# A Mamba block beside a two-layer local transformer: P's transposes in row halves, and six summed groups of eight

## The chip, the cores and the metric

The kernel runs on one core of a Trainium2 chip. The core has TensorE (PE, whose weight loads are shown as PEld), VectorE (DVE), ScalarE (ACT), GpSimd (POOL) and SyncE (SP), which issues nearly all DMAs here. The metric is the time of one execution on the device in microseconds (us). Everything is computed in float32.

## The reference

The input x has 4096 tokens of 256 features. Two branches read it, and the result is the sum that the kernel forms from x and both branches' contributions.

The Mamba branch, on the normalized tokens: a projection to 512 inner channels and a gate, a causal convolution of 4 taps with SiLU, then a state of 16 numbers per channel:

```
dt  = softplus(dt_lr @ dt_w.T + dt_b)
dA  = exp(dt * A)                     # per channel and state
h_t = dA_t * h_(t-1) + dt * x_conv * B
y_t = sum over the 16 states of h_t * C_t
out = ((y + x_conv * D) * silu(z)) @ out_w.T
```

The transformer branch has two layers. In each, tokens are shifted by half of their features and projected to q, k and v of 8 heads of 64. q and k are normalized and rotated. Attention is local: a window of 128 queries sees its own 128 keys and the 128 before, with a mask. After it come an output projection with a residual, a layer norm and a gated MLP.

```
sim  = q @ k.T                        # 128 x 256 per head and window, masked
attn = softmax(sim)                   # "P" below
o    = attn @ v
```

## The kernel before

**Tiling.** A transformer step handles 256 tokens (two windows) of one layer; there are 16 steps in each of 2 layers. The Mamba branch goes in 8 blocks of 512 tokens, each in 4 chunks of 128 channels: 32 chunk-blocks, one beside each transformer step. All of it is one program in which the instructions of both branches are interleaved.

**What sets the order.** Each operation is handed to a planner by `add(engine, us, emit, reads, writes, ..., soon=...)`. `us` is the duration that the planner assumes, and `soon` is a lead: the operation's due time is moved ahead by it (or back, where it is negative). A list scheduler then plays the five engines and picks on each the operation that is due first among those whose inputs and buffers are ready. `AHEAD` says how far ahead of the oldest unfinished work an operation may be due to be considered. For PE, `part` says how the array is used: the whole of it (""), two halves of its rows ("rows") or of its columns ("columns"). The planner charges `SWITCH` (0.1) for a change and prefers work of the same part within `NEAR` (0.3). The resulting order is written out for each engine and is fixed: an engine does not pass a waiting instruction. All of SP's DMAs stand in one such order too.

**Mamba's states** (`recur`, L772 on). A chunk-block takes its 16 states in 8 groups of two. For each group SP loads two 512 KB buffers (`bc`, seven in all) with B and C spread over the partitions. GpSimd multiplies B by dt*x (L793, 128x1024). For each of the two states ACT computes the decay (L802), DVE scans (L807) and multiplies by C into the first buffer (L817). The sum over states is taken by PE: four transposes of 128x128 a state accumulate into one PSUM bank `y` (L829). In groups named in `PAIRED` GpSimd adds the two states first (L825), and PE has four transposes instead of eight. `PAIRED` is (1, 3, 5, 7). `close` copies y out and finishes the chunk.

**Attention** (`attend`, `pair(g)`). A window's 8 heads go in two pairs of head pairs, g = 0 and 1. For each g:

- `score` (L1017): products for four heads with contraction 64, two at a time in the halves of the array's rows, into two PSUM banks.
- `masked` (L1032, DVE): mask, scale and row maximum. `soft` (L1042, ACT): exponential and row sum, into the SBUF tiles `prs[j]`, each with queries as partitions and two heads x 256 keys.
- `turn` (L1055): P's transposes, 128x128, so that the keys become partitions. It is done for each head pair i on its own: four transposes (two heads, two pieces of keys) into one PSUM bank, whole array.
- an ACT copy of each bank into an SBUF tile `prT` (L1059; four tiles in all).
- `mix` (L1071): products with v, two at a time in halves of the columns.

Five PSUM banks named `mm` serve all products of both branches, two hold decays and one holds `y`. A float32 product that isn't a transpose leaves two records in the trace for one written instruction; a transpose leaves one.

Of the kernel before, what the change touches and what calls it, by code (L numbers as in the profile page):

```python
# [42 lines left out]
AHEAD = 2.32  # L43
# [5 lines left out]
PAIRED = (1, 3, 5, 7)  # L49
# [269 lines left out]
def mamba_and_local_transformer(  # L319
# [45 lines left out]
    probs_T = buffer("prT", 4, [P, 2, 2, P])  # L365
# [89 lines left out]
    def load_small():  # L455
        dma(96, lambda: xpw.ap, lambda: xp_wT.rearrange("(c p) n -> p c n", p=P), writes=[xpw], soon=-0.84)
        for at_row in (0, DH):
            dma(32, lambda at_row=at_row: dtw.ap[at_row : at_row + DTR], lambda: dt_wT, writes=[(dtw, at_row)], soon=-0.13)
        dma(128, lambda: b2row.ap, lambda: b2_d[DEPTH - 1 : DEPTH, :].partition_broadcast(P), writes=[b2row], soon=-0.82)

    def load_qkv(l):
        for s in range(3):
            cut = slice(s * INNER, (s + 1) * INNER)
            dma(
                512, lambda cut=cut: wqkv.ap[:, :, cut],
                lambda cut=cut: wqkv_d[l][:, cut].rearrange("(k p) n -> p k n", p=P), writes=[(wqkv, s)], soon=-0.17,
            )

    def load_rest(l):
        dma(512, lambda: wo.ap, lambda: wo_d[l].rearrange("(h p) n -> p h n", p=P), writes=[wo], soon=0.41)  # L470
        for half in range(2):
            for m, n in ((0, WHOLE), (NM - 1, LAST)):
                to, of = w1_at(half, m), half * HID + m * MC
                dma(
                    n, lambda to=to, n=n: w1.ap[:, :, to : to + n],
                    lambda of=of, n=n: w1_d[l][:, of : of + n].rearrange("(k p) n -> p k n", p=P),
                    writes=[(w1, (half, m))], soon=-1.5,
                )
# [3 lines left out]
            lambda: w2_d[l][0:whole, :].rearrange("(m p) n -> p m n", p=MC), writes=[(w2, 0)], soon=0.34,  # L482
        )
        dma(42, lambda: w2.ap[0 : HID - whole, NM - 1, :], lambda: w2_d[l][whole:HID, :], writes=[(w2, 1)], soon=0.91)
# [28 lines left out]
        add("PE", 8.3, shift, [w1], [pb], soon=-0.76)  # L513
        add("DVE", 0.4, bias, [pb], [b1, b1x], soon=-0.11)
        add("DVE", 4.6, scale, [], [w1], port=True, soon=-1.45)
# [14 lines left out]
    def base_of(s):  # L530

        base = plan.value(rows_b)
        if s in sums:
            dma(256, lambda: base.ap, lambda: sums[s].ap, [sums[s]], [base], soon=-0.77)
            return base
        dma(256, lambda: base.ap, lambda: rows(x, s), writes=[base], soon=-1.13)
# [3 lines left out]
            ), [b2row], [base], soon=-0.58,  # L540
# [3 lines left out]
    def finish(s, po, base):  # L544

        add("DVE", 0.6, lambda: nc.vector.tensor_tensor(base.ap, halves(po), base.ap, ALU.add), [po], [base], soon=-1.06)
        if s in sums:
            dma(256, lambda: rows(out, s), lambda: base.ap, [base], soon=-0.55)
            return
        sums[s] = plan.fixed(dram.tile([P, NW, D], F32, tag=f"sum{s}", name=f"sum{s}"))  # L550
        dma(256, lambda: sums[s].ap, lambda: base.ap, [base], [sums[s]], soon=-1.4)
# [4 lines left out]
    def shift_column(l, s):  # L556
        now = xts[l, s]
        if s == 0:
            add("POOL", 0.14, lambda: nc.gpsimd.memset(now.ap[:, 1, 0:1], 0.0), [], [(now, 0)], soon=-0.51)
        else:  # L560
# [3 lines left out]
                [(old, 1)], [(now, 0)], soon=-0.73,  # L564
            )

    def normalize(s):
# [5 lines left out]
        dma(256, lambda: xb.ap, lambda: rows(x, s), writes=[xb], soon=0.15)  # L573
# [27 lines left out]
        add("DVE", 1.1, stats, [xb], [mv], soon=1.5)  # L601
        add("ACT", 0.5, root, [mv], [rstd], soon=0.26)
        add("DVE", 0.6, centre, [mv, rstd], [xb], port=True, soon=0.02)
        now = xts[0, s] = plan.value(tokens)
        add("PE", 0.44, turn, [xb], [pt], holds=[now], soon=0.92)
        add("ACT", 0.48, lambda: nc.scalar.copy(now.ap[:, :, 1:], halves(pt)), [pt], [(now, 1)], soon=0.26)
        shift_column(0, s)
        dma(256, lambda: xn_d[s].ap, lambda: now.ap[:, :, 1:], [(now, 1)], [xn_d[s]], soon=0.98)
# [3 lines left out]
    def reload(s):  # L612
        now = xts[1, s] = plan.value(tokens)
        dma(256, lambda: now.ap[:, :, 1:], lambda: x1_d[s].ap, [x1_d[s]], [(now, 1)], soon=0.04)
        shift_column(1, s)
# [5 lines left out]
    def in_half(i):  # L621
# [3 lines left out]
            lambda: in_wT[:, i * DI : (i + 1) * DI].rearrange("(k p) n -> p k n", p=P), writes=[w], soon=-1.17,  # L625
# [3 lines left out]
    def in_proj(b, w, c, to):  # L629
# [9 lines left out]
        add("PE", 1.72, emit, [w, xms[b]], [pm], holds=[to], soon=-0.68)  # L639
        return pm  # L640

    def front_load(b):
        xm = xms[b] = plan.value(xms_b)
        for i in range(PB):
            s = b * PB + i
            dma(
                256, lambda i=i: xm.ap[:, :, i * TS : (i + 1) * TS], lambda s=s: xn_d[s].ap, [xn_d[s]], [(xm, i)], soon=0.54
# [5 lines left out]
    def front_conv(b, c, w):  # L653
        xin, xc, tail = plan.value(rows_m), xcs[b], tails[b]
        edge = slice(c * (TAPS - 1), (c + 1) * (TAPS - 1))
        if b == 0:
            add("POOL", 0.14, lambda: nc.gpsimd.memset(xin.ap[:, 0 : TAPS - 1], 0.0), [], [(xin, 0)], soon=-0.13)
        else:
# [3 lines left out]
                [(old, c)], [(xin, 0)], soon=0.95,  # L662
            )
        pm = in_proj(b, w, c, xin)
        add("ACT", 0.48, lambda: nc.scalar.copy(xin.ap[:, TAPS - 1 :], pm.ap), [pm], [(xin, 1)], soon=1.39)
        if b < NB - 1:
            add(
                "POOL", 0.14, lambda: nc.gpsimd.tensor_copy(tail.ap[:, edge], xin.ap[:, TB:]), [(xin, 1)], [(tail, c)], soon=-0.13
# [5 lines left out]
            ), [], [pm], soon=-1.0,  # L674
# [8 lines left out]
        for j in range(TAPS - 1):  # L683
            add("DVE", 0.7, lambda j=j: tap(j), [xin, pm], [(xc, c) if j == TAPS - 2 else pm], soon=1.04)

    def silu(v):
# [4 lines left out]
        add("ACT", 4.52, emit, [], [v], soon=0.84)  # L691

    def front_dbl(b):
# [3 lines left out]
        def emit():  # L697
# [9 lines left out]
        add("PE", 1.75, emit, [xc, xpw], [px], holds=[xd, part], soon=-0.37, part="columns")  # L707
        add("ACT", 0.48, lambda: nc.scalar.copy(part.ap[0:n, 0:TB], px.ap[DH : DH + n]), [px], [part], alone=[px], soon=-0.04)
        add(
            "DVE", 0.6, lambda: nc.vector.tensor_tensor(xd.ap[0:n], px.ap[0:n], part.ap[0:n, 0:TB], ALU.add),  # L710
            [px, part], [(xd, 0)], alone=[px], soon=-1.5,
        )

        add("ACT", 0.48, lambda: nc.scalar.copy(xd.ap[DH : DH + DTR], xd.ap[0:DTR]), [(xd, 0)], [(xd, 1)], soon=-0.52)
        xds[b] = xd
        bc = bcs[b] = plan.fixed(dram.tile([2 * NS, TB], F32, tag=f"bc{b}", name=f"bc{b}"))
        dma(64, lambda: bc.ap, lambda: xd.ap[DTR:n, :], [(xd, 0)], [bc], soon=-0.16)
# [8 lines left out]
    def times(b, c):  # L726
# [12 lines left out]
        add("PE", 1.15, emit, [xd, dtw], banks2, holds=dts2, soon=1.25, part="rows")  # L739
        for i in range(2):  # L740
# [3 lines left out]
                ), [banks2[i]], [dts2[i]], soon=0.16,  # L744
# [3 lines left out]
    def prepare(b, c):  # L748

        if c % 2 == 0:  # L750
# [7 lines left out]
        add("ACT", 0.6, lambda: nc.scalar.activation(e.ap[:, n], dt.ap, AF.Abs), [dt], [e], soon=-0.49)  # L758
        add("ACT", 0.6, lambda: nc.scalar.activation(dt.ap, dt.ap, AF.Relu), [], [dt], soon=-1.5)
        add("ACT", 0.54, lambda: nc.scalar.activation(e.ap[:, n], e.ap[:, n], AF.Exp, scale=-1.0), [], [e], soon=0.5)  # L760
        add(
            "DVE", 0.36, lambda: nc.vector.tensor_scalar(r.ap[:, n], e.ap[:, n], 1.0, -1.0, ALU.add, ALU.add),
            [e], [r], port=True, soon=-0.19,
        )
        add("POOL", 1.22, lambda: nc.gpsimd.tensor_tensor(r.ap[:, n], e.ap[:, n], r.ap[:, n], ALU.subtract), [e], [r], soon=-0.36)
        add("ACT", 0.6, lambda: nc.scalar.activation(e.ap[:, n], e.ap[:, n], AF.Ln, bias=one_t), [], [e], soon=-0.3)
        add("POOL", 1.22, lambda: nc.gpsimd.tensor_tensor(dt.ap, dt.ap, r.ap[:, n], ALU.add), [r], [dt], soon=-1.41)
        add("POOL", 1.22, lambda: nc.gpsimd.tensor_tensor(dt.ap, dt.ap, e.ap[:, n], ALU.add), [e], [dt], soon=-0.94)
        add(
            "DVE", 0.61, lambda: nc.vector.tensor_tensor(dtx.ap, dt.ap, xc.ap[:, c, :], ALU.mult),  # L770
            [dt, (xc, c)], [dtx], port=True, soon=0.7,
# [3 lines left out]
    def recur(b, c, g):  # L775
# [6 lines left out]
        for s in range(2):  # L782
# [4 lines left out]
                .rearrange("n t -> (n t)").partition_broadcast(P), [bc], [w], soon=-0.76,  # L787
# [7 lines left out]
            ), [dtx], [u], soon=-0.28,  # L795
        )
        for i in range(NG):
# [6 lines left out]
                ), [dt], [h], soon=0.0,  # L804
# [4 lines left out]
                ), [(u, i), (state, (c, n))], [h], soon=-1.02,  # L809
            )  # L810
            if b < NB - 1:
                add(
                    "ACT", 0.1, lambda h=h, n=n: nc.scalar.copy(state.ap[:, c, n : n + 1], h.ap[:, TB - 1 : TB]),  # L813
                    [h], [(state, (c, n))], alone=[h], soon=0.11,
# [4 lines left out]
                ), [h, spread[1]], [(u, i)], alone=[h], soon=-0.32,  # L819
# [4 lines left out]
        if n_sums == 1:  # L824
            add("POOL", 1.22, lambda: nc.gpsimd.tensor_tensor(u.ap[:, 0, :], u.ap[:, 0, :], u.ap[:, 1, :], ALU.add), [], [u], soon=-1.1)  # L825
# [13 lines left out]
        for i in range(n_sums):  # L839
            add("PE", 0.44, lambda i=i: collect(i), [(u, i)], [y], soon=-0.01)  # L840

    def close(b, c):
# [3 lines left out]
        add("ACT", 0.48, lambda: nc.scalar.copy(ytv(), y.ap), [y], [yt], soon=-0.43)  # L846

        def turn():
# [3 lines left out]
        add("PE", 0.44, turn, [yt], [py], soon=-0.55)  # L852
# [3 lines left out]
            ), [py], [(xc, c)], soon=-0.04,  # L856
# [3 lines left out]
            [sz], [(xc, c)], soon=-0.23,  # L860
        )

    def out_load():
# [3 lines left out]
            writes=[w], soon=-1.42,  # L867
# [3 lines left out]
    def out_proj(b, i, w):  # L871
# [12 lines left out]
        add("PE", 3.44, emit, [w, xc, base], [po], soon=-1.12)  # L884
# [5 lines left out]
    def rotation(l, s):  # L890
# [3 lines left out]
            writes=[rot], soon=-0.47,  # L894
        )
        for i, scales in enumerate((qks, qkw)):
            for q in range(2):
# [6 lines left out]
                    ), [rot], [(trig, (i, q))], soon=-0.44,  # L904
# [3 lines left out]
    def project(l, s, t):  # L908
# [3 lines left out]
        def matmuls(q, holds):  # L912
# [10 lines left out]
            add("PE", 1.72, emit, [xb, (wqkv, q)], [pm], holds=holds, soon=0.27)  # L923
# [4 lines left out]
        def norm(q, pm, sq):  # L928
            add("ACT", 0.48, lambda: nc.scalar.activation(sq.ap, pm.ap, AF.Square), [pm], [sq], alone=[pm], soon=0.56)
# [3 lines left out]
                ), [sq], [(nrm, q)], soon=-0.65,  # L933
# [10 lines left out]
        def turned(parts, to):  # L944
            add("POOL", 1.22, lambda: nc.gpsimd.tensor_tensor(parts[0].ap, parts[0].ap, parts[1].ap, ALU.add), [parts[1]], [parts[0]], soon=0.5)  # L945
# [476 lines left out]
```

## Time and profile before

| | |
|---|---|
| median of 3 runs | 1888.05 us (1886.05 to 1889.43) |
| profiled execution | 1890.55 us, its span 1888.8 us |
| mean granted TensorE clock | 0.992 |
| DVE L807, the scans | 448 x 1279 ns, 563.7 us |
| POOL L793, products with B | 256 x 2368 ns, 605.7 us |
| ACT L1059, copies of the transposed P | 256 x 595 ns, 133.9 us |
| PE L1017, scores | 2016 records, 135.4 us busy |
| SP waiting for L829 / L817 to release a buffer | 499.4 / 645.5 us |
| DMA | 334.69 MB, 177 GB/s |

A group line of the page has: line, engine, operation, what is written from what, shapes and count; then busy time and the mean duration of one in ns; then the engine's idle time just before such instructions and what ended most of it. PE's instructions are pipelined, so their mean duration is a latency and not the distance from one to the next.

### The profile page before, as it was taken

Reading aid. Unit: us, or ns where it says so; the run is one execution under the profiler, and the core shown is the slowest. Engines: PE = TensorE matmul, PEld = TensorE weight load, DVE = VectorE, ACT = ScalarE, POOL = GpSimd, SP = SyncE. Lnnn points to the kernel's source line nnn. Section 1 sums busy time; section 2 is a strip of 40 time slices with the busy share of each in tenths; the row PEclk is TensorE's granted clock in tenths of the full one; section 3 lists DMA queues with packets and bytes.
Section 4 is the critical chain, followed back from the end, with each engine's and each line's share of the span. In section 5 each row is a group of like instructions: output and inputs, shape, how many; then the busy total and the mean of one; then the engine's idle time right before and its main releaser. Section 6 shows DMA issues by size and latency. Waiting matters only on the chain. (4 is left out here: it accounts for less than half of the span.)

```text
span 1888.8 us, 35786 instructions
## 1 busy us (share of the span) xinstructions
PE 1850.9 (98%) x12432; PEld 1422.4 (75%) x12432; DVE 1667.1 (88%) x3030; ACT 1588.7 (84%) x3794; POOL 1508.6 (80%) x1274
## 2 busy tenths in 40 slices
PE   7999999999999999999999999999999999999997
PEld 4777767777777777778778787787778777787886
DVE  6688898899898999988899888989889898899886
ACT  5788888888898888897896979988798888988793
POOL 4578778887887778887888787988788987798885
PEclk9899999999999999999999999999999999999999
DMA  5354555565455555556555554556544575455564
GB/s 189 125 193 131 171 167 167 178 209 179 157 176 190 181 179 185 164 186 208 166 186 204 181 191 147 187 170 209 176 147 171 176 248 169 144 173 175 193 197 142
DMA packets 133956, 334.69 MB, mean 177 GB/s; under 512 B 13468, under 2 KB 57200, under 8 KB 133776
## 3 DMA queue, kind: packets, MB, share of 16 engines
q1 hardware_dynamic: 133488, 332.21, 53.1%
q8 instruction: 98, 1.61, 0.3%
q14 instruction: 82, 0.67, 0.1%
q10 hardware_dynamic: 288, 0.20, 0.0%
HBM read 315.06 MB, written 17.30 MB: 176 GB/s over the span
## 5 line engine op out<-in xcount | busy, mean ns | idle before, releaser
L793 POOL TENSOR_TENSOR bc<-dtx,bc 128x1024 f32<-128x1024 f32 x256 | 605.7, 2368 | 80.7 <-DMA bc<-bc 44.7
L807 DVE TENSOR_TENSOR_SCAN da<-da,state,bc 128x512 f32<-128x512 f32 x448 | 563.7, 1279 | 56.6 <-ACT da L802 32.8
L802 ACT ACTIVATE da<-dt,negA 128x512 f32<-128x512 f32 x512 | 349.2, 698 | 49.7 <-DVE bc L817 47.9
L918 PE MATMUL mm<-wqkv,xt 128*128 128x512 f32 x768 | 353.5, 598 | 1.4 <-DVE top L1032 0.8
L817 DVE TENSOR_TENSOR bc<-da,bc 128x512 f32<-128x512 f32 x512 | 338.3, 679 | 5.8 <-ACT state L813 3.7
L1176 PE MATMUL mm<-hn,w 128*128 128x256 f32 (+1 forms) x1408 | 329.2, 381 | 2.1 <-DVE top L1032 0.7
L1176 PEld LDWEIGHTS mm<-hn,w 128*128 128x128 f32 (+1 forms) x1408 | 256.1, 188 | 39.1 <-DVE top L1032 1.6
L1042 ACT ACTIVATE pr<-pr,top 128x256 f32<-128x256 f32 (+1 forms) x512 | 253.3, 501 | 10.6 <-DVE top L1032 10.4
L918 PEld LDWEIGHTS mm<-wqkv,xt 128*128 128x128 f32 x768 | 139.7, 191 | 137.0 <-issue 121.2
L1032 DVE CUSTOM_DVE_ANT_0 pr<-mm,maskf,nrm 128x256 f32<-128x256 f32 (+1 forms) x512 | 212.4, 473 | 14.5 <-PE mm L1017 13.7
L825 POOL TENSOR_TENSOR bc<-bc 128x512 f32<-128x512 f32 x128 | 165.3, 1291 | 71.5 <-DVE bc L817 65.2
L829 PE MATMUL y<-ident,bc 128*128 128x128 f32 x1536 | 219.6, 277 | 2.2 <-ACT m2k L846 1.5
L985 POOL TENSOR_TENSOR turn<-turn,trig 128x512 f32<-128x512 f32 x128 | 162.4, 1288 | 74.0 <-DVE turn L978 63.0
L829 PEld LDWEIGHTS y<-ident,bc 128*128 128x128 f32 x1536 | 177.1, 141 | 58.6 <-issue 40.0
L945 POOL TENSOR_TENSOR turn<-turn,turn 128x512 f32<-128x512 f32 x128 | 164.2, 1283 | 32.4 <-DVE turn L965 31.4
L1017 PEld LDWEIGHTS mm<-kT,qT 64*128 64x128 f32 x2016 | 119.7, 187 | 30.9 <-issue 21.9
L1221 POOL TENSOR_TENSOR mlp<-mlp,ga 128x512 f32<-128x512 f32 (+2 forms) x128 | 127.2, 1008 | 19.1 <-ACT ga L1233 10.0
L1059 ACT COPY prT<-mm 128x512 f32<-128x512 f32 (+1 forms) x256 | 133.9, 595 | 3.4 <-PE mm L1055 3.1
L1017 PE MATMUL mm<-kT,qT 64*128 64x128 f32 x2016 | 135.4, 280 | 0.0
L1071 PE MATMUL mm<-prT,v 128*64 128x128 f32 x2016 | 134.5, 281 | 0.0
L1071 PEld LDWEIGHTS mm<-prT,v 128*64 128x64 f32 x2016 | 113.8, 137 | 25.1 <-issue 8.8
L1055 PE MATMUL mm<-ident,pr 128*128 128x128 f32 x1008 | 130.5, 276 | 2.0 <-ACT qT L956 0.9
(132 smaller groups left out, 3499.4 us busy)
## 6 DMA issues: line engine op xcount, KB each, us to landing
bc<-bc SPq DMA_DIRECT2D x512, 512.0 KB, 4.5
io<-in_x SPq DMA_DIRECT2D x32, 256.0 KB, 5.4
mw<-in_in_wT SPq DMA_DIRECT2D x16, 512.0 KB, 4.8
rot<-in_rot SPq DMA_DIRECT2D x32, 128.0 KB, 4.2
xn<-xt SPq DMA_DIRECT2D x16, 256.0 KB, 3.6
xm<-xn SPq DMA_DIRECT2D x16, 256.0 KB, 4.4
x<-mid SPq DMA_DIRECT2D x16, 256.0 KB, 4.6
mw<-in_out_wT SPq DMA_DIRECT2D x8, 512.0 KB, 6.1
```

Source lines behind the costliest of these rows:

```text
L793: "POOL", 2.35, lambda: nc.gpsimd.tensor_tensor(u.ap, dtx.ap.unsqueeze(1).to_broadcast([P, NG, TB]), u.ap, ALU.mult), [dtx], [u], soon=-0.28,
L802: "ACT", 0.63, lambda h=h, n=n: nc.scalar.activation(h.ap, dt.ap, AF.Exp, scale=negA[:, c * NS + n : c * NS + n + 1]), [dt], [h], soon=0.0,
L807: "DVE", 1.18, lambda h=h, n=n, i=i: nc.vector.tensor_tensor_scan(h.ap, h.ap, u.ap[:, i, :], state.ap[:, c, n : n + 1] if b else 0.0, ALU. ...
L817: "DVE", 0.61, lambda h=h, i=i: nc.vector.tensor_tensor(u.ap[:, i, :], h.ap, spread[1].ap[:, i, :], ALU.mult), [h, spread[1]], [(u, i)], a ...
L825: add("POOL", 1.22, lambda: nc.gpsimd.tensor_tensor(u.ap[:, 0, :], u.ap[:, 0, :], u.ap[:, 1, :], ALU.add), [], [u], soon=-1.1)
L829: nc.tensor.matmul(y.ap[:, t, :], lhsT=u.ap[:, i, t * P : (t + 1) * P], rhs=ident, is_transpose=True, start=g == 0 and i == 0 and t == 0, ...
L918: nc.tensor.matmul(pm.ap, lhsT=hT[k], rhs=wqkv.ap[:, k, q * INNER : (q + 1) * INNER], start=k == 0, stop=k == KC - 1,)
L1017: nc.tensor.matmul(halves(scs[j])[:, i, a * WIN : (a + 1) * WIN], lhsT=qT.ap[half, 2 * g + i, :], rhs=kk.ap[half, 2 * g + i, :], start=n == 0,
L1032: nc.vector.tensor_tensor_reduce(out=prs[j].ap[:, i, keys], in0=halves(scs[j])[:, i, keys], in1=mask[:, keys], scale=nrm.ap[:, h : h + 1], ...
L1042: nc.scalar.activation(prs[j].ap[:, i, keys], prs[j].ap[:, i, keys], AF.Exp, bias=top.ap[:, h : h + 1], scale=-1.0, accum_out=den.ap[:, h ...
L1071: nc.tensor.matmul(hpair(po.ap)[j * DH : (j + 1) * DH, hp, :], lhsT=vv.ap[:, h * DH : (h + 1) * DH], rhs=prT.ap[:, j, a, :], start=a == first,
L1176: nc.tensor.matmul(halves(pm)[0:r, i, :], lhsT=w1.ap[:, k, c0 : c0 + r], rhs=hn.ap[:, k, :], start=k == 0, stop=k == KC - 1,)
```

## The change

P's transposes: `turn` now handles both head pairs of a g in one piece of work. Each transpose of 128 queries x 128 keys becomes two of 64 queries x 128 keys, one in each half of the array's rows (partitions 0 to 63 and 64 to 127), written to two different banks. Bank r holds the queries of half r for both head pairs, both heads and both pieces of keys. The two ACT copies each take one bank and write every 64-query half into one wide `prT` (two tiles of twice the size instead of four). The planner's price for the turn is 0.62 as a "rows" piece, where it was twice 0.44 for the whole array.

Sums: `PAIRED` gets the groups 0 and 4, so GpSimd adds in six groups of eight. `AHEAD` goes from 2.32 to 2.82. The leads (`soon`) of nearly every operation are set anew; no operation is added or removed by that.

```diff
-AHEAD = 2.32
+AHEAD = 2.82
...
-PAIRED = (1, 3, 5, 7)
+PAIRED = (0, 1, 3, 4, 5, 7)
...
-    probs_T = buffer("prT", 4, [P, 2, 2, P])
+    probs_T = buffer("prT", 2, [P, 2, 2, 2, P])
...
-            prTs = []
-            for i in range(2):
-                pp, prT = plan.value(banks), plan.value(probs_T)
-                ppv = lambda pp=pp: pp.ap.rearrange("p (j a q) -> p j a q", j=2, a=2)
-
-                def turn(i=i, ppv=ppv):
+            pps, prT = [plan.value(banks) for _ in range(2)], plan.value(probs_T)
+            ppv = lambda r: pps[r].ap.rearrange("p (i j a q) -> p i j a q", i=2, j=2, a=2)
+
+            def turn():
+                for i in range(2):
                     for j in range(2):
                         for a, _, _ in pieces:
-                            nc.tensor.transpose(ppv()[:, j, a, :], prs[j].ap[:, i, a * WIN : (a + 1) * WIN], ident)
-
-                add("PE", 0.44, turn, prs, [pp], holds=[prT], soon=0.0)
+                            for r in range(2):
+                                half = slice(r * DH, (r + 1) * DH)
+                                nc.tensor.transpose(
+                                    ppv(r)[:, i, j, a, :], prs[j].ap[half, i, a * WIN : (a + 1) * WIN], ident[half, half]
+                                )
+
+            add("PE", 0.62, turn, prs, pps, holds=[prT], soon=1.35, part="rows")
+            for r in range(2):
                 add(
-                    "ACT", 0.48, lambda ppv=ppv, prT=prT: nc.scalar.copy(prT.ap[:, :, first:], ppv()[:, :, first:]),
-                    [pp], [prT], soon=0.27,
+                    "ACT", 0.48, lambda r=r: nc.scalar.copy(
+                        prT.ap[:, :, :, first:, r * DH : (r + 1) * DH], ppv(r)[:, :, :, first:, :]
+                    ), [pps[r]], [(prT, r)], soon=1.4,
                 )
...
             add(
-                "PE", 1.0, mix, prTs + [vv for _, _, vv in pieces], [(po, g)], holds=[] if g else [OT], soon=1.25,
+                "PE", 1.0, mix, [prT] + [vv for _, _, vv in pieces], [(po, g)], holds=[] if g else [OT], soon=0.0,
                 part="columns",
             )
```

## The prediction

> **What bounds the kernel now.** I read the page's engine shares first, then busy time and granted clock in windows of 200 us, then what TensorE waited for, then TensorE's instructions in order of time.
>
> ```profile
> PE 1850.9 (98%) x12432; PEld 1422.4 (75%) x12432; DVE 1667.1 (88%) x3030; ACT 1588.7 (84%) x3794; POOL 1508.6 (80%) x1274
> ...
> L829 PE MATMUL y<-ident,bc 128*128 128x128 f32 x1536 | 219.6, 277 | 2.2 <-ACT m2k L846 1.5 <-POOL bc L825 0.7
> ...
> L825 POOL TENSOR_TENSOR bc<-bc 128x512 f32<-128x512 f32 x128 | 165.3, 1291 | 71.5 <-DVE bc L817 65.2 <-DVE nrm L972 4.0 <-DVE den L1088 2.1
> ...
> L1055 PE MATMUL mm<-ident,pr 128*128 128x128 f32 x1008 | 130.5, 276 | 2.0 <-ACT qT L956 0.9 <-ACT kT L956 0.5 <-ACT state L813 0.4
> ```
>
> PE has work in 98% of the span and its groups show almost no idle time; 24 us of its 38 idle us lie in the first 100 and the last 189. So what counts is PE's own work. The means of 276 ns are latencies of pipelined instructions. The pace must be read from starts, in the timeline of TensorE (start, duration, instruction, count):
>
> ```profile
> 899.35 2.06 PE L1017 MATMUL mm<-kT,qT 64*128 64x128 f32 x32
> 901.34 0.66 PE L829 MATMUL y<-ident,bc 128*128 128x128 f32 x4
> ...
> 910.57 1.04 PE L1055 MATMUL mm<-ident,pr 128*128 128x128 f32 x8
> 911.44 0.60 PE L829 MATMUL y<-ident,bc 128*128 128x128 f32 x4
> 911.88 1.04 PE L1055 MATMUL mm<-ident,pr 128*128 128x128 f32 x8
> 912.84 1.15 PE L1071 MATMUL mm<-prT,v 128*64 128x128 f32 x16
> 913.92 0.66 PE L829 MATMUL y<-ident,bc 128*128 128x128 f32 x4
> 914.50 1.15 PE L1071 MATMUL mm<-prT,v 128*64 128x128 f32 x16
> ```
>
> Eight transposes take 911.44 - 910.57 = 0.87 us, 109 ns each. The next eight take 0.96 until L1071 starts: 0.09 more, because L1071 puts two products side by side in the array's columns[...]. Scores (L1017, side by side in rows) go in pairs, 112 ns a pair. Every change between whole array, rows and columns shows the same 93 ns in the starts. And the first load behind a change isn't hidden. Windows that hold only the first instruction show it:
>
> ```profile
> 913.92 0.33 PE L829 MATMUL y<-ident,bc 128*128 128x128 f32 x1
> ```
> ```profile
> 899.35 0.37 PE L1017 MATMUL mm<-kT,qT 64*128 64x128 f32 x1
> ```
>
> Their usual durations are 0.27. So a load of 128 columns for a transpose costs 0.055 us, one for a plain product 0.10 us; L1071's, of 64 columns, 0.05 (0.32 against 0.27).
>
> With these paces (512 moving columns 429 ns, 256: 216, 128: 109 to 112) I add up PE's instructions in the order of the program: 1760.7 us of work, and 361 changes of the array at 93 ns + 72 ns of exposed load on average, 59.6 us. Sum 1820.3. The span is 1888.8, so 68.5 us are left: 24 idle at the ends, some 13 at half clock (clock 0.95, 0.99, 0.98 and 0.98 in four of the windows), and 31 us of short waits.
>
> **The change, part by part.**
>
> *Six groups of eight summed by GpSimd.* Two more groups per chunk and block, 32 chunk-blocks: 64 times four transposes of L829 go, 256 x 109 ns = 27.9 us off PE. POOL gets 64 x 1291 ns = 82.6 us and comes to 1591 us. It was idle 380 us, so the sum lies beside PE's work; it isn't free: in groups 0 and 4 the buffer of products is released by PE one sum later (1.3 us and POOL's queue), and SP's loads into those buffers wait for just such releases (499 us behind L829, 645 behind L817). SP is in order, so the loads of tokens, weights and rotations stand behind them. POOL's products L793 already waited 44.7 us for these loads. PE's waits for L825's sums were 3.3 us in 128 sums, 5 with 192.
>
> *P's transposes in row halves.* Before: 1008 x 109 = 109.9 us. After: 2016 transposes of 64 rows and 64 moving columns, two at a time: 1008 pairs. No row of the trace has such a pair. From below: 64 columns stream in 55 ns (half of 109), and the load of 128 columns takes 55. From above: 112 ns, the scores' pair. Here a rule speaks against the change. The Trainium skill, "TensorE: Matmul & The Clock Gate", section "LDWEIGHTS (loading the stationary operand)", says that a load costs its number of columns over 1.2 ns, whatever the number of rows: 107 ns for 128 columns. Half the rows are still 128 columns, and the trace has a place where this load alone sets the pace, the bias products with one moving column:
>
> ```profile
> 1013.51 2.29 PE L495 MATMUL mm<-cols,w 128*128 128x1 f32 x20
> ```
>
> 2.29 less 0.25 for the last one, over 19 steps, is 107 ns. By the rule the pairs cost 1008 x 112 = 112.9 us and nothing is gained. But L495 is a plain product; the row of a transpose's load is the 0.33 against 0.27 above, half the rule's price. The changed instruction is a transpose, so I take 58 ns: the distance of the first two loads of L829 at 913.92 and 913.97, rounded up for the 7 ns by which the second half follows the first. 1008 x 58 = 58.5 us: 51.4 less. Both ends, 56 and 112, go into the range.
>
> *The price: changes of the array.* The transposes were whole-array work that could stand beside any of the other transposes and products; now they are row work. Counted over the two programs' order of matmuls, 361 changes become 576: the 128 turns stand alone in the rows 91 times, in twos 12 times, next to scores or L734 some ten times. 215 x 165 ns = 35.3 us back. Per lone turn: 0.87 before; 0.46 + two times 0.093 + an exposed load of 0.055 before and 0.055 to 0.10 behind, 0.76 to 0.81 after. The row halves alone thus win only 16 us.
>
> *Two banks at once, one wide prT.* A turn now starts only when two of the five banks are free; before each half took one. The ACT copies stay 256 of 512 elements (595 ns each, 133.9 us), with 64-element runs in what they write; ACT is 84% busy, so a few per cent there (5 us) would lie beside PE. L1071's products waited for both copies before and do so now. Taking a free bank from another unit can cost a wait, or by a luckier order save one: +-6 us.
>
> *Leads.* They change the order on all engines and SP; no instruction is added, and AHEAD lets work start from further ahead. Removed waits can be at most the 31 us; a worse order can cost as much. Nearest row: the waits now. They should grow, since the other engines' idle time shrinks: at 1850 us DVE is 90% busy (88 now), ACT and POOL 86 (84 and 80). Waits in proportion to the inverse of idle time grow by a fifth (DVE) to 40% (POOL): 31 us become 37 to 43. I take +8. DVE's instructions that stand behind POOL (L762: 408 ns at best, 871 on average; L770: 659 and 939) cost DVE 24 us now, and some 1.5 more with POOL's larger share.
>
> *Sum.* PE's work: 1760.7 - 27.9 - 51.4 = 1681.4; changes 94.9; sum 1776.2, 44.1 less than before. Span 1888.8 - 44.1 + 8 = 1852.7. The profiled execution took 1890.55 and the median of three runs is 1888.05, 0.75 below the span; so **1852 us**.
>
> **Rivals.**
> 1. *The load sets the pace of the row halves*, by the rule and L495. Place: the 1008 pairs; price 54 ns a pair more than I take, 54.4 us. PE's sum is then 1830.6, 10 us over the old one: 1888 + 10 + a few us of waits = **1900 us, slower**. It decides from 102 ns a pair on (58 + 44.1 us / 1008). For it: L495, and the scores' 112. Against: the exposed load of transposes, 55 ns, in every change into L829. Chance 0.11.
> 2. *GpSimd and the buffers of products.* POOL's 82.6 us aren't absorbed: late sums hold back releases, SP's loads land late, L793 waits and DVE's scans run dry. For it: 44.7 us of waits of L793 for loads, SP waiting most of the time. Against: seven buffers, and 380 us of idle POOL. If four tenths of it reach PE, +33 us less the 8 already counted: **1877 us**; if all of it does, it is slower by some 38. Chance 0.17, of which 0.04 slower and 0.05 no change.
> 3. *The order gets better.* A longer look ahead takes away a third of the 31 us instead of adding 8: **1834 us**. For it: all leads are set together with the new costs. Against: every engine is fuller. Chance 0.12.
> 4. *The change doesn't do what it says*, rows serialised in the array rather than side by side: 1008 x 2 x 55 = 111 us, which is rival 1's time. The scores' pairs speak against it; its chance is in rival 1's.
>
> **How the numbers follow.** Forecast 0.60, rivals 0.11, 0.17, 0.12. The forecast's own range is 1840 to 1866 (56 to 70 ns a pair, waits -4 to +12). The range for 8 in 10 takes in rival 2's price and rival 3's near half: 1834 to 1886. About 0.2%, 4 us, is what a measurement of this kernel can tell from no change. Faster: 0.60 + 0.12 + 0.08 of rival 2 = 0.80; within: 0.05; slower: 0.11 + 0.04 = 0.15.
>
> **What would show it.** Right: turns of 16 transposes in about 0.46 us between first and last start; L829 at 1280; 192 sums in L825 and POOL near 1590 us; PE still at 97 to 98% of a shorter span. Wrong: pairs at 107 to 112 ns; waits of PE for L825 or of L793 for loads well over 10 and 45 us; PE's share falling to 95%; or more half clock[...].

## The result and the profile after

The changed kernel is slower: 1915.15 us (median of 4 runs, 1910.42 to 1925.15) against 1888.74; the ratio is 1.0147, 95% interval 1.0104 to 1.0190. The profiled execution took 1925.15 us, the longest of the four, with a span of 1923.4; the others lie 10 to 15 us lower, so some 10 us of what its profile shows is not typical.

The page of the changed kernel, shares of the span and the groups that answer to those of before:

```profile
PE 1842.9 (96%) x13184; PEld 1372.9 (71%) x13184; DVE 1702.8 (89%) x3030; ACT 1590.6 (83%) x3794; POOL 1583.6 (82%) x1338
...
L825 POOL TENSOR_TENSOR bc<-bc 128x512 f32<-128x512 f32 x192 | 244.9, 1280 | 80.1 <-DVE bc L817 72.2
...
L829 PE MATMUL y<-ident,bc 128*128 128x128 f32 x1280 | 186.2, 280 | 10.5 <-DVE bc L817 4.3
```

and two turns in the timeline of TensorE:

```profile
899.77 1.17 PE L1116 MATMUL mm<-OT,wo 128*128 128x128 f32 x9
900.87 0.71 PE L1057 MATMUL mm<-ident,pr 64*128 64x64 f32 x16
901.51 1.98 PE L635 MATMUL mm<-xm,mw 128*128 128x512 f32 x4
903.43 0.71 PE L1057 MATMUL mm<-ident,pr 64*128 64x64 f32 x16
904.07 0.70 PE L1145 MATMUL mm<-sq,mean_w 128*128 128x256 f32 x2
```

The counts are as forecast: 1280 transposes of L829, 192 sums, POOL at 1584 us. A turn takes 0.64 us up to the next start. Less 0.09 for the change of the array and 0.055 for the exposed load, that is 0.495 for eight pairs, 62 ns a pair; inside all the turns, too, the distance from one pair to the next is 62 ns at the median. PE's work did shrink: with 62 ns its sum (work and changes of the array) is 1780.3 us, 40 less than the 1820.3 of before. But what the span has beyond that sum grew from 68.5 to 143.1 us (some 133 at the median time).

A part of this growth is the clock. The same 32 products take nearly twice as long where the granted clock is 0.50 (second line) as at full clock:

```profile
906.01 2.02 PE L1075 MATMUL mm<-prT,v 128*64 128x128 f32 x32
...
1647.67 3.73 PE L1075 MATMUL mm<-prT,v 128*64 128x128 f32 x32
```

By the mean clock the changed kernel lost at most (1 - 0.984) x 1923.4 = 31 us to this, the kernel before (1 - 0.992) x 1888.8 = 15. As an estimate, then, up to 16 us of the 75 are half clock. PE's idle time, by the shares of the two pages, grew from 38 to 80 us.

VectorE gained 36 busy us with the same instructions. Its smallest ones show where (line, instruction, count; busy, mean ns; idle before), first the kernel before, then the changed one:

```profile
L972 DVE TENSOR_SCALAR nrm<-nrm 128x16 f32<-128x16 f32 x64 | 22.2, 346 | 0.2
L770 DVE TENSOR_TENSOR dtx<-dt,xc 128x512 f32<-128x512 f32 x32 | 30.0, 939 | 3.7 <-POOL dt L768 2.8 <-POOL bc L793 0.9
```
```profile
L972 DVE TENSOR_SCALAR nrm<-nrm 128x16 f32<-128x16 f32 x64 | 42.7, 668 | 0.2
L770 DVE TENSOR_TENSOR dtx<-dt,xc 128x512 f32<-128x512 f32 x32 | 37.6, 1176 | 2.6 <-POOL bc L793 2.6
```

L972 works on 16 elements; in the changed kernel its shortest run is 110 ns and its longest 4648, which is about two of GpSimd's products L793 (2367 ns). Here is one that took 2.31 us, and the GpSimd product beside it:

```profile
915.73 2.31 DVE L972 TENSOR_SCALAR nrm<-nrm 128x16 f32<-128x16 f32 x1
...
915.65 2.35 POOL L793 TENSOR_TENSOR bc<-dtx,bc 128x1024 f32<-128x1024 f32 x1
```

They end within 0.04 us of each other. All 24 of the L972s over 0.4 us (11 in the kernel before) end within 0.25 us of the end of a GpSimd instruction. So a VectorE instruction that stands behind GpSimd counts as busy while it stands.

### The profile page after: what moved, and what is told of

It is laid out like the page before. It is cut to its first block, busy times and chain, and to the rows that moved or that the text cites. A ratio compares the mean times of both kernels' runs of the same rounds, so it can differ in the third digit from the quotient of the medians.

```text
span 1923.4 us, 37415 instructions
## 1 busy us (share of the span) xinstructions
PE 1842.9 (96%) x13184; PEld 1372.9 (71%) x13184; DVE 1702.8 (89%) x3030; ACT 1590.6 (83%) x3794; POOL 1583.6 (82%) x1338
## 5 line engine op out<-in xcount | busy, mean ns | idle before, releaser
L793 POOL TENSOR_TENSOR bc<-dtx,bc 128x1024 f32<-128x1024 f32 x256 | 605.2, 2367 | 89.0 <-DMA bc<-bc 60.2
L918 PE MATMUL mm<-wqkv,xt 128*128 128x512 f32 x768 | 365.2, 602 | 4.4 <-DVE OT L1105 1.1
L1180 PE MATMUL mm<-hn,w 128*128 128x256 f32 (+1 forms) x1408 | 317.3, 382 | 4.3 <-DVE hn L1171 4.3
L825 POOL TENSOR_TENSOR bc<-bc 128x512 f32<-128x512 f32 x192 | 244.9, 1280 | 80.1 <-DVE bc L817 72.2
L1180 PEld LDWEIGHTS mm<-hn,w 128*128 128x128 f32 (+1 forms) x1408 | 262.6, 190 | 46.1 <-DVE hn L1171 6.3
L918 PEld LDWEIGHTS mm<-wqkv,xt 128*128 128x128 f32 x768 | 134.4, 191 | 122.0 <-issue 107.0
L829 PE MATMUL y<-ident,bc 128*128 128x128 f32 x1280 | 186.2, 280 | 10.5 <-DVE bc L817 4.3
L829 PEld LDWEIGHTS y<-ident,bc 128*128 128x128 f32 x1280 | 146.6, 142 | 46.5 <-issue 18.6
L1017 PE MATMUL mm<-kT,qT 64*128 64x128 f32 x2016 | 142.9, 283 | 8.3 <-ACT sq L929 2.9
L1075 PE MATMUL mm<-prT,v 128*64 128x128 f32 x2016 | 138.7, 284 | 6.5 <-ACT state L813 2.8
L813 ACT COPY state<-da 128x1 f32<-128x1 f32 x448 | 71.8, 166 | 73.3 <-DVE da L807 60.9
```

The costliest lines, as they stand in the source:

```text
L793: "POOL", 2.35, lambda: nc.gpsimd.tensor_tensor(u.ap, dtx.ap.unsqueeze(1).to_broadcast([P, NG, TB]), u.ap, ALU.mult), [dtx], [u], soon=-0.29,
L829: nc.tensor.matmul(y.ap[:, t, :], lhsT=u.ap[:, i, t * P : (t + 1) * P], rhs=ident, is_transpose=True, start=g == 0 and i == 0 and t == 0, ...
L918: nc.tensor.matmul(pm.ap, lhsT=hT[k], rhs=wqkv.ap[:, k, q * INNER : (q + 1) * INNER], start=k == 0, stop=k == KC - 1,)
L1017: nc.tensor.matmul(halves(scs[j])[:, i, a * WIN : (a + 1) * WIN], lhsT=qT.ap[half, 2 * g + i, :], rhs=kk.ap[half, 2 * g + i, :], start=n == 0,
L1075: nc.tensor.matmul(hpair(po.ap)[j * DH : (j + 1) * DH, hp, :], lhsT=vv.ap[:, h * DH : (h + 1) * DH], rhs=prT.ap[:, i, j, a, :], start=a == ...
L1180: nc.tensor.matmul(halves(pm)[0:r, i, :], lhsT=w1.ap[:, k, c0 : c0 + r], rhs=hn.ap[:, k, :], start=k == 0, stop=k == KC - 1,)
```

## The experiments

Two kinds of kernel were run. In the first kind the planner gets what it got, so each engine's order and all places in the queues stay, and only what is written at a place changes. In the second kind the leads are searched anew: a few leads at a time are changed at random and kept when the end of the planner's own schedule moves forward. These searches had different lengths and starts, so a few us between them mean little.

### The changed kernel's order with the old instructions

`a1_whole` writes P's transposes as before at the turn's place, one head pair to a bank:

```diff
-                            for r in range(2):
-                                half = slice(r * DH, (r + 1) * DH)
-                                nc.tensor.transpose(
-                                    ppv(r)[:, i, j, a, :], prs[j].ap[half, i, a * WIN : (a + 1) * WIN], ident[half, half]
-                                )
+                            nc.tensor.transpose(whole(i)[:, j, a, :], prs[j].ap[:, i, a * WIN : (a + 1) * WIN], ident)
```

> The changed kernel's order on every engine and its leads are kept; only P's transposes are written as 128x128 on the whole array again, one head pair a bank. PE's work grows by 51 us and loses about 200 changes of the array (33 us): some +16 us. Theory 'order' (the new order holds the waits, whatever the instructions): 1915 + 10 to 20 = 1925 to 1935 us. Theory 'row halves' (their two banks, their drains or short pieces make the waits): at or below 1900 us. Theory 'GpSimd' expects no gain either: 1915 to 1930 us.

`a2_unsummed` leaves GpSimd's sum out in groups 0 and 4 and gives PE both states there:

```diff
-lambda: nc.gpsimd.tensor_tensor(u.ap[:, 0, :], u.ap[:, 0, :], u.ap[:, 1, :], ALU.add)
+lambda: g in (0, 4) or nc.gpsimd.tensor_tensor(u.ap[:, 0, :], u.ap[:, 0, :], u.ap[:, 1, :], ALU.add)
...
-            add("PE", 0.44, lambda i=i: collect(i), [(u, i)], [y], soon=0.0)
+            add("PE", 0.44, lambda i=i: [collect(n) for n in ((0, 1) if g in (0, 4) else (i,))], ...)
```

> The changed kernel's order is kept; groups 0 and 4 aren't summed on GpSimd, and PE takes eight transposes for them at the place where it took four. POOL has 82 us less, PE 28 us more. Theory 'GpSimd' (its sums hold back buffers, and VectorE stands behind it at the shared port: L972 went from 347 to 667 ns, L770 from 939 to 1175): faster than the changed kernel by 15 to 35 us, 1880 to 1900. Theory 'order': 0 to 28 us slower, 1915 to 1943.

`a3_both` has both edits, hence the instructions of the kernel before in the changed kernel's order.

> The changed kernel's order with the instructions of the kernel before: whole-array transposes and four summed groups. What is left against the kernel before is the order alone (leads and AHEAD, and the places planned for the two parts). Theory 'order': 1925 to 1955 us, PE's waits still 100 us or more. If the two parts themselves make the waits: near 1889 us.

| in the changed kernel's order | us | ratio to before |
|---|---|---|
| old instructions (a3_both) | 1930.01 | 1.0217 (1.0192 to 1.0242) |
| row halves alone (a2_unsummed) | 1922.69 | 1.0183 (1.0157 to 1.0208) |
| six sums alone (a1_whole) | 1914.62 | 1.0138 (1.0118 to 1.0158) |
| both (the changed kernel) | 1915.15 | 1.0147 (1.0104 to 1.0190) |

The changed kernel's order costs 41 us with the old instructions, as theory "order" expected of a3_both (1925 to 1955). It isn't the leads alone: in this order a turn still takes two banks at once and does both head pairs in one piece, and PE takes both states of groups 0 and 4 in one piece. What these pieces cost apart from the leads wasn't measured. At least 16 us are the leads: r_after, below, keeps all instructions and pieces of the changed kernel, has other leads, and is that much faster.

In this order the six sums alone bring 15 us. The row halves alone bring 7, which the spread of four runs each doesn't tell from nothing, and on top of the sums they bring nothing (1915.15 against 1914.62). Of 44 us of PE's work only 15 arrive. a1_whole hit none of its theories: it is 10 us under what "order" expected, and far above "row halves".

Theory "GpSimd" expected a2_unsummed to be 15 to 35 us faster than the changed kernel. It was 7 slower, within the spread; but PE had 28 us more in exchange, so this judges the exchange and not GpSimd's 82 us by themselves.

What may eat the row halves' gain is seen in the waits: PE's loads for the turns, in a1_whole (whole array) and in the changed kernel (row halves), both in the same order.

```profile
PEld mm L1055 <- ACT pr L1042: 5.0, 11, 0.8
```
```profile
PEld mm L1057 <- ACT pr L1042: 9.5, 21, 0.8
```

These are the largest lines (total us, times, longest). All waits of such loads for other engines come to 11 us in 24 places in a1_whole and to 35 us in 71 places in the changed kernel. The row halves take some 16 us off PE's sum. The loads overlap PE's work, so not each of these waits holds PE up, and some may be the change of the array, which that sum counts already. So this is not shown to be the cause.

The rise of VectorE's busy time belongs mostly to the order: with old instructions and GpSimd at its old 1508 us it is 1693 already (1667 before).

```profile
PE 1866.3 (97%) x12432; PEld 1428.1 (74%) x12432; DVE 1692.7 (88%) x3030; ACT 1593.4 (83%) x3794; POOL 1507.7 (78%) x1274
```

### VectorE behind GpSimd

`a4_nomax` is the changed kernel without L972; the lower bound on the norms is left out.

```diff
-        add("DVE", 0.08, lambda: nc.vector.tensor_scalar_max(nrm.ap, nrm.ap, NORM_MIN**2), [], [nrm], port=True, soon=-0.62)
+        add("DVE", 0.08, lambda: None, [], [nrm], port=True, soon=-0.62)
```

> The changed kernel without L972, the lower bound on the squared norms (64 VectorE instructions of 16 elements that stand behind GpSimd's at a mean of 667 ns, 42.7 us in all). The order of all others is the same. If this standing behind GpSimd is what PE waits for: 15 to 40 us faster, 1875 to 1900. If it lies beside other work: 0 to 8 us faster.

1905.74 us, ratio 1.0078 (1.0056 to 1.0100): some 9 us faster than the changed kernel. VectorE's busy time fell by 39 us (1702.8 to 1663.7), so a quarter of it reached the end: just over the 0 to 8 us of work that lies beside other work, and under the 15 to 40 of a single cause.

`b_bound` does the same in the kernel before without losing the bound: it becomes a bias of the logarithm that follows on ScalarE.

```diff
-            nc.scalar.activation(nrm.ap, nrm.ap, AF.Ln, scale=65536.0)
+            nc.scalar.activation(nrm.ap, nrm.ap, AF.Ln, scale=65536.0, bias=bound_t)
```

> The kernel before, its order kept; L972 is gone, and its lower bound on the squared norms is the bias of the logarithm that follows on ScalarE. VectorE has 22 us less, most of it standing behind GpSimd. As a part of the net: 2 to 6 us faster, 1884 to 1888. If PE alone sets the time: no change.

1887.97 against 1889.14 us, ratio 0.9992 (0.9985 to 0.9999): about 1 us, less than expected, and the only full computation here that is faster than the kernel before at all.

### Are leads and AHEAD one fitted set?

`ahead_alone` is the kernel before with one number changed:

```diff
-AHEAD = 2.32
+AHEAD = 2.82
```

> The kernel before with AHEAD 2.82 instead of 2.32 and all of its own leads. If leads and AHEAD are one fitted set (theory 'order'): slower by 40 us or more, over 1930 us, with the same instructions. If a longer look ahead is harmless or good in itself: 1880 to 1895 us.

1980.18 us, ratio 1.0474 (1.0450 to 1.0497). The same instructions are 90 us slower, double what was expected at least. At most 28 of these are half clock, by the mean clock of 0.978 against 0.992. The leads of the kernel before belong to its AHEAD.

### What is PE's work worth?

All kernels of this section keep the order of the kernel before. `s1_pe` takes 128 x 4 transposes from PE:

```diff
         def collect(i):
-            for t in range(NT):
+            for t in range(0 if i else NT):
```

> The kernel before, its order kept, with 55.8 us less of PE's work (128 x 4 transposes of L829): groups 0, 2, 4 and 6 give PE only their first state, so half of their states is missing from y. Theory 'PE' (the prediction's basis: PE's own work sets the time): 1835 to 1845 us. Theory 'net' (each engine works its fixed order off at 80 to 98% load and they wait for each other, so work taken from one comes back only in part): 1860 to 1880 us.

1879.36 us, ratio 0.9938 (0.9917 to 0.9959): of 56 us taken from an engine at 98%, some 11 arrive. That is the slow end of what "net" expected, and "PE", the prediction's ground, falls. PE's sum is now 1764.0, the span 1877.6, so 113.6 us are left where 68.5 were. What PE's loads waited for, first before, then in s1_pe (total us, times, longest):

```profile
PEld mm L1071 <- ACT prT L1059: 6.4, 29, 0.8
PEld mm L918 <- DVE top L1032: 6.1, 18, 0.9
PEld mm L950 <- POOL turn L945: 5.1, 10, 1.3
```
```profile
PEld mm L950 <- POOL turn L945: 15.0, 29, 1.3
...
PEld mm L918 <- DVE top L1032: 11.4, 27, 1.1
...
PEld mm L1071 <- ACT prT L1059: 7.4, 28, 0.8
```

No single wait took the place of PE's work. It came back as short ones, on GpSimd, on VectorE and on ScalarE, none of those shown longer than 1.3 us.

`s3_dve` reads 8 of each head's 64 features for the norms (L931), `s4_pool` sums 128 of 512 columns in L825; the rest of both is left out.

```diff
-sq.ap.rearrange("p (h d) -> p h d", d=DH), AX.X, ALU.add
+sq.ap.rearrange("p (h d) -> p h d", d=DH)[:, :, 0:8], AX.X, ALU.add
```

> The kernel before, its order kept, with some 70 us less of VectorE's work: the 128 sums for the norms (L931) read 8 of each head's 64 features. Theory 'PE': within 5 us of 1889. Theory 'net': 10 to 30 us faster, 1860 to 1880.

```diff
-nc.gpsimd.tensor_tensor(u.ap[:, 0, :], u.ap[:, 0, :], u.ap[:, 1, :], ALU.add)
+nc.gpsimd.tensor_tensor(u.ap[:, 0, 0:P], u.ap[:, 0, 0:P], u.ap[:, 1, 0:P], ALU.add)
```

> The kernel before, its order kept, with some 110 us less of GpSimd's work: the 128 sums of L825 take 128 of 512 columns, the rest of those sums is left out. Theory 'PE': within 5 us of 1889. Theory 'net': 5 to 25 us faster.

1887.16 (ratio 0.9982, 0.9975 to 0.9989) and 1886.13 us (0.9977, 0.9963 to 0.9990). VectorE had 48 us less (1619.3) and GpSimd 102 (1406.1); each alone brought 3 to 4 us. Both numbers are what theory "PE" expected (within 5 us) and miss "net", while s1_pe missed "PE". So neither theory holds as it was put: lightening any one of the three in this order brings little.

`s7_pe_dve` joins s1_pe and s3_dve. `s6_all` lightens PE and GpSimd as above, and squares and sums only 128 of 512 columns for the norms, which lightens ScalarE and VectorE.

> The kernel before, its order kept, PE lighter by 56 us and VectorE by some 50 us as in s1_pe and s3_dve. If VectorE is the second bound: 1840 to 1855. If not: 1870 to 1878, s1_pe and s3_dve added.

> The kernel before, its order kept, lighter on all four at once: PE 56 us (as s1_pe), VectorE some 60 us (norms' sums read 128 of 512 columns), ScalarE some 40 us (squares of 128 of 512 columns), GpSimd some 100 us (as s4_pool). Theory 'net': 30 to 55 us faster, 1835 to 1860, since nobody waits for anybody's old pace. Theory 'fitted order' (places in the queues, not loads, hold it): 1865 to 1880, little under s1_pe.

1867.39 (0.9886, 0.9871 to 0.9900) and 1854.02 us (0.9810, 0.9791 to 0.9828). PE's 56 us and VectorE's 48 together bring 22, where on their own they brought 11 and 3; that is a little more than their sum, and far from what a second bound on VectorE would give (1840 to 1855). With all four lighter it is 35, as "net" expected. The page of s6_all:

```profile
PE 1802.5 (97%) x11920; PEld 1368.2 (74%) x11920; DVE 1617.6 (87%) x3030; ACT 1549.9 (84%) x3794; POOL 1405.7 (76%) x1274
```

PE is at 97% here and in s1_pe (1815.1 us), and at 96% in the slower changed kernel. The share of busy time hardly tells these apart. The changed kernel's PE is shown idle for 80 of its 1923.4 us, but 143 are left beyond its sum: the rest, short waits and half clock, lies inside what is shown as busy.

`s2_sums` was to put the sums of groups 0 and 4 into the old order:

```diff
+                if i and g in (0, 4):
+                    nc.gpsimd.tensor_tensor(u.ap[:, 0, :], u.ap[:, 0, :], u.ap[:, 1, :], ALU.add)
...
-            add("PE", 0.44, lambda i=i: collect(i), [(u, i)], [y], soon=-0.01)
+            add("PE", 0.44, lambda i=i, late=late: [collect(0)] * i if late else collect(i), [(u, i)], [y], soon=-0.01)
```

> The kernel before, its order and leads kept, with the sums of groups 0 and 4 put on GpSimd behind the second product (64 x 1.28 us) and four transposes instead of eight. PE has 27.9 us less, POOL 82 us more. Theory 'PE': 1860 to 1870 us. Theory 'net': 1880 to 1900, as PE now waits for the sums and POOL's later works come later.

As written it takes the first state's transposes in both places, once before the sum and once behind it, so PE got no lighter, and the sums wait for PE as well as PE for them. It took 1943.16 us (ratio 1.0276, 1.0261 to 1.0292). It doesn't test what it was meant to; it shows only that 82 us of GpSimd's work with its waits, at places that no plan made for them, cost 53 us.

### Leads fitted to each set of instructions

`r_after`, `r_before`, `r_sums` (six sums, whole-array transposes), `r_halves` (row halves, four sums) and `r_pe` (s1_pe's instructions, with the planner told of them) have new leads and a new AHEAD (2.73, 2.41, 2.56, 2.39 and 2.37); beyond that only what is named here differs from the kernel before or the changed one. `r_after_nosum` keeps r_after's order and leaves out GpSimd's sums, and so the second state, in groups 0 and 4.

> The changed kernel (row halves, six summed groups) with its leads searched further against its own planner; nothing else changes. Theory 'order' (the changed kernel's leads, not its parts, cost the 41 us that its order costs with the old instructions): at or below the kernel before, 1865 to 1890 us, with PE's short waits down by 25 us or more. Theory 'parts' (two banks at once and GpSimd's sums make waits that no order avoids): 1900 us or more.

> The kernel before with its leads searched further in the same way; the instructions are the old ones. It shows what a search alone is worth. Theory 'order': 1875 to 1895 us, since this kernel's PE has only some 30 us of waits to give. If it lands far above 1889 us, a search against the planner doesn't carry over to the chip, and r_after says nothing.

> Six summed groups of eight, P's transposes on the whole array as before, leads searched for this. PE has 28 us less than before at the same number of changes of the array. Theory 'order': 1860 to 1885 us, at least as fast as r_after, because the row halves return most of their gain in changes of the array. If GpSimd's sums hold the rest back: 1890 us or more.

> s1_pe's instructions (half of the states of groups 0, 2, 4 and 6 left out, PE 55.8 us lighter, nothing added anywhere), with the planner told so and the leads searched anew for it. Theory 'fitted order' (in the old order the others hold PE back, in a fitted one they needn't): 1835 to 1855 us. Theory 'other engines' (VectorE, ScalarE and GpSimd at 80 to 88% are the bound whatever the order): 1870 us or more.

> Row halves alone (four summed groups as before), leads searched for it. PE has 51 us less of transposes and about 30 us more of array changes. If row halves cost nothing else: 1878 to 1888 us. If their two banks at once and the short pieces make waits of their own: 1892 us or more, as slow as or slower than r_before's 1893.

> r_after, its order kept, without GpSimd's sums of groups 0 and 4 (the second state of these groups is left out; PE's work stays as in r_after). Theory 'GpSimd' (its 82 us take the gain): 15 us or more faster than r_after's 1899, at or below 1884. Theory 'row halves' (their short pieces and two banks at once take it): within 7 us of r_after.

PE's sum is worked out as in the prediction, with 62 ns a pair in row halves; "left" is the profiled span less this sum.

| | PE's sum | left | us | ratio to before |
|---|---|---|---|---|
| before | 1820.3 | 68.5 | 1889 | 1 |
| r_before | 1817.3 | 71.3 | 1893.50 | 1.0017 (1.0010 to 1.0024) |
| r_pe | 1765.3 | 81.9 | 1853.14 | 0.9809 (0.9789 to 0.9829) |
| r_sums | 1793.1 | 92.3 | 1891.70 | 1.0013 (1.0003 to 1.0023) |
| r_halves | 1802.8 | 88.1 | 1900.69 | 1.0058 (1.0041 to 1.0075) |
| r_after | 1779.6 | 115.0 | 1898.76 | 1.0038 (1.0024 to 1.0052) |
| r_after_nosum | 1779.6 | 110.0 | 1896.17 | 1.0036 (1.0021 to 1.0051) |
| changed kernel | 1780.3 | 143.1 | 1915.15 | 1.0147 (1.0104 to 1.0190) |

The profiled executions are not all typical: r_halves' was the fastest of its runs (1892.65 us) and the changed kernel's the slowest, so at the median "left" is some 96 and 133 us there.

r_pe is the counterpart of s1_pe: the same lighter PE, but with an order fitted to it, brings 36 us instead of 11, without relief for any other engine, as theory "fitted order" expected. The search alone brought nothing: r_before is 3 us slower than the kernel before. Its page:

```profile
PE 1799.9 (97%) x11920; PEld 1365.0 (74%) x11920; DVE 1675.7 (91%) x3030; ACT 1581.4 (86%) x3794; POOL 1507.9 (82%) x1274
```

So the other engines' load isn't a wall at 1889 us: here VectorE runs at 91%. A fitted order is worth 16 us to the changed kernel (1915 to 1899), but doesn't take it under the kernel before: neither of r_after's two theories hits, its 1899 lies between their numbers. The row halves alone, fitted, come out slower than r_before by 7 us although PE's sum is 14 us smaller, as the theory of waits of their own expected: the loads of its turns wait 22 us for other engines, those of r_before 7. The sums alone, fitted, leave r_sums and r_before within 2 us, though PE's sum is 24 us smaller. That is what was expected if GpSimd's sums hold the rest back (1890 us or more, where "order" had 1860 to 1885), but no run separates it from a less lucky search. r_after_nosum says that GpSimd's sums aren't what holds r_after in its given order; since s1_pe showed that lightening one engine in a given order says little, this doesn't clear them in an order made without them.

## Why the prediction was wrong

- **The pace of the pairs was right.** I took 58 ns and it was 62, from the exposed load of a transpose (0.49 us between a turn's first and last start, 0.46 said), against the 112 of the scores and of a rule on loads. Rival 1 is out.
- **Counts were right:** 576 changes, 1280 transposes, GpSimd at 1584 us (1591 said). A lone turn was to cost 0.76 to 0.81 us with all its edges. Shown are 0.64 to the next start and 0.09 ahead; with the next load's 0.055 to 0.10 that is 0.78 to 0.83.
- **"So what counts is PE's own work" was the first step to fail.** It was read from 98% busy. s1_pe measured it: in the old order 56 us of PE's work are worth 11. In the changed kernel's order the parts' 44 us were worth 15, all of which the sums bring alone.
- **"Leads: I take +8" was the second, and about as large** (33 us off, against 29 of the first). The term reckoned with how full the engines are. The order itself was the unknown: with the old instructions it costs 41 us (a3_both, the larger pieces included; at least 16 of it are leads, by r_after), and one number of it can cost 90 (ahead_alone). "A worse order can cost as much" as the 31 us of waits was too small a bound. Together: 1889 + 41 - 15 = 1915. Why this order is worse, wait by wait, stays open.
- **VectorE behind GpSimd**, put at 1.5 us more: L972, L770, L589 and L762 gained 30 us together (20.5, 7.6, 5.5 and -4.0). The Trainium skill, "SBUF — State Buffer", section "SBUF: two separate sides", says of GpSimd and of some kinds of VectorE instructions that the pair of ports which they share is an exclusive lock for a whole instruction, and that the other one is blocked outright; L972's 110 to 4648 ns, and their ends beside GpSimd's, agree. What that is worth at the end was 9 us for L972 (a4_nomax). It was priced from GpSimd's share, but it depends on where the instruction stands in the order.
- **Rival 2** (GpSimd's sums aren't absorbed) is not what happened in this order, where the sums gained 15 us, or 7 within the spread beside the row halves. Its sign, L793's waits for loads, did grow, from 44.7 to 60.2 us; but with the old instructions in the same order they are 96.9 (a3_both), so they come with the order and not with the sums. In fitted orders the rival stays open: r_pe's 56 us bring 36 with nothing added, r_sums' 28 bring about 2 with 82 us added on GpSimd.
- **More half clock** was named as a sign, and came. The mean clock fell from 0.992 to 0.984 in the profiled run and was 0.985 to 0.988 in the others: 8 to 16 us more than before at most, of the 26 by which the kernel is slower. In a3_both (0.989 to 0.991) it is some 6 at most, so the order's 41 us are mainly waits. The row halves alone don't bring it: r_halves has 0.989 to 0.993.

Not settled: how much more than 16 of the 41 us is leads, and how much the larger pieces; how much of r_halves' loss is the two banks at once and how much the shorter pieces or the search; whether a longer search would bring the changed kernel under 1889 us; and GpSimd's part in a fitted order.

## What to carry to other kernels

An engine that shows 98% busy in a program of in-order queues is the bound only if lightening it moves the end: take some of its work out with the order kept, and look, before pricing a change by its work. Where an order was fitted by a search to one set of instructions and durations, price the order as a part of the change, with the spread of such orders as its bound. To tell the two apart, write the old instructions at the new order's places.

## What was not expected

- The same instructions took from 1889 to 1980 us by one planner constant.
- In the old order 102 us less on GpSimd or 48 on VectorE are worth 3 to 4 us each, 56 on PE 11, and all together, with 39 on ScalarE, 35.
- The clock was 0.984 to 0.988 in every run of the kernels with both parts (the changed kernel, a4_nomax, r_after) and 0.987 to 0.993 in those with one part or none, but for ahead_alone (0.978 and 0.981). So neither the row halves nor the sums explain it alone; what does was not tried.
